# Moving the column maxima from TensorE to VectorE in a transformer block, and bunching the first MLP product

## The chip, the cores and the metric

The kernel runs on one core of a Trainium2 chip. The time is the device time of one execution in microseconds (us); lower is better. Several runs are taken and their median is used. One more execution is recorded by the hardware profiler; all spans, waits and durations below are from it. The engines are called by their names in the profile: PE (TensorE matmul), PEld (its weight loads), DVE (VectorE), ACT (ScalarE), POOL (GpSimd) and SP (SyncE, which here only issues DMAs).

## What is computed

A transformer block with conditioning, for 2 sequences of 2048 tokens, 576 channels, 16 heads of 36, all in fp32:

```python
ada = silu(c) @ W_ada + b_ada
shift_msa, scale_msa, gate_msa, shift_mlp, scale_mlp, gate_mlp = split(ada, 6)
h = layernorm(x) * (1 + scale_msa) + shift_msa
q, k, v = heads(h @ W_qkv + b_qkv)
o = softmax(q * 36 ** -0.5 @ k.T) @ v
x = x + gate_msa * (o @ W_proj + b_proj)
h = layernorm(x) * (1 + scale_mlp) + shift_mlp
x = x + gate_mlp * (gelu(h @ W_fc1 + b_fc1) @ W_fc2 + b_fc2)
```

The softmax needs, for each query, the maximum over 2048 keys. The MLP is 2304 wide, 18 chunks of 128.

## The kernel before

**Front.** The first part computes the conditioning rows in six parts (`rows_of`, products `pa`), and queries, keys and values of the first sequence. The generator `later` holds the conditioning parts 2 to 5 and the scaling of the projection weights by the gates. It is advanced by one `yield` for each step of the other work. Its bare `yield`s are all that sets where on PE the third part (`gates(2, g1)`, L425 on PE) stands.

**Main loop.** The attention is cut into 128 units, one for each head and each block of 512 queries (8 blocks of 16 heads). A unit has NG = 4 groups of 512 keys, and one turn of the loop, a slot, is one group. So slot g of a unit is one of 0 to 3. In slot G the loop emits, in this order:

- scores of the group eight slots ahead (`scores`, L648, 64x64 tiles, keys on the partitions, queries along the row), into two PSUM buffers of two banks, `ps_s`
- their copies to SBUF on ACT (`keep`, L661)
- filler on PE, if the slot is to have some (`fill`)
- the exponentials of the next slot's group on ACT (`exps`, L707)
- the last, 64-row part of the filler (`last`, `quads`, L104)
- weighting of the values with this slot's exponentials (`weigh`, L719, 64x64 tiles)
- on DVE the subtraction of the maximum from the group two slots ahead (`less`, L703) and the running maximum over keys of the new scores (`maxima`, L666)
- `flush()`, what was put off by a slot, then the eviction of the filler, then at a unit's last slot `take` (L731, L732), which adds the two halves of the weighted sum.

Every engine works through its instructions in the order written (`seq`). PE thus waits in `scores` for `keep` of the slot before, and in `weigh` for an exponential, which waits for a subtraction.

**The maximum.** After the fourth group, `acc` holds for each partition a maximum of each query over a part of the keys (twice 512 queries, folded into 512). What is left is a maximum across the 128 partitions. It is made one slot later (`chain`): `turn` transposes four 128x128 pieces on PE into one of the `ps_s` buffers (L684), `across` reduces them on DVE (L694), writes the 512 maxima to memory and reads them back spread over all partitions as `m` (L695, L698, both on SP's queue). The subtraction wants `m` two slots after that. SP's queue also carries the keys and queries of the next unit but one (`load_keys`, issued when a unit starts) and half of the stores of a unit's output (`store`).

**Filler.** What is not attention is cut into steps with a cost on PE: queries, keys and values of the second sequence (`projections`), and for each finished block the projection, the second norm and the MLP (`block`). Each slot adds RATE = 2.51 to a credit, each step takes its cost from it. Before, a slot takes a step if g is even, or if the credit is over RATE; the credit starts at -32. In the MLP, `up_to(f)` makes two chunks of the first product: four 128-row products for chunk 0 (cost 4.29, with the 64-row rest of both chunks), and, as a step of its own, four for chunk 1 (3.43). Then come the biases (L1183), a square (L1190), a DVE product (L1192), and one slot later tanh (L1198) and another product (L1200). `down` makes the second product (L1220, cost 5.94). These fillers use two PSUM banks, `ps_f`. The transposes of the normed tokens (`lights`) are put into slots that have no other filler.

**Closing loop.** When the last unit is done, the rest of the filler runs alone.

Of the kernel before, what the change touches and what calls it, by code (L numbers as in the profile page):

```python
# [10 lines left out]
F32 = mybir.dt.float32  # L11
AF = mybir.ActivationFunctionType
# [10 lines left out]
def dit_block_kernel(  # L23
# [150 lines left out]
    with ExitStack() as front:  # L174
# [342 lines left out]
        def later():  # L517

            was[2] = load_ada(2)
            was[5] = load_ada(5)  # L520
            lines = ap.tile([P, C], F32, name="lines")
            for b in range(B):
                for i, src in enumerate((b_fc2, b_proj)):
                    at = ds(64 * b + 32 * i, 1)
                    seq(nc.gpsimd.dma_start(out=lines[at, :], in_=src.unsqueeze(0)))
            yield
            yield
            yield
            pas[2] = cleared(2)
            yield  # L530
            g1 = []
            yield from gates(2, g1)
            was[3] = load_ada(3)
            pas[5] = cleared(5)
            yield
            g2 = []
            yield from gates(5, g2)
            was[4] = load_ada(4)
            half = [ap.tile([P, C], F32, name=f"half_{b}") for b in range(B)]
            for b in range(B):  # L540
                seq(nc.vector.tensor_scalar_mul(half[b], g2[b], 0.5))
                for i, (to, g) in enumerate(((gb_d, g2), (gp_d, g1))):
                    at = ds(64 * b + 32 * i, 1)
                    seq(nc.vector.tensor_mul(lines[at, :], lines[at, :], g[b][at, :]))
                    seq(nc.gpsimd.dma_start(out=to[b].unsqueeze(0), in_=lines[at, :]))
            yield
            split = lambda w: [
                (pieces(w)[0][:, kc : kc + 2, :], P, 2) for kc in range(0, KC - 1, 2)
            ] + [(w[(KC - 1) * P : C].unsqueeze(1), KL, 1)]
            to = [split(wpr_d[b]) for b in range(B)]  # L550
            jobs = [
                (*job, g1, [to[b][i][0] for b in range(B)])
                for i, job in enumerate(split(w_proj))
            ]
            src = w_fc2.rearrange("(f p) n -> p f n", p=P)
            dsts = [w2_d[b].rearrange("(f p) n -> p f n", p=P) for b in range(B)]
            for f in range(0, NF, 3):
                at = slice(f, f + 3)
                jobs.append((src[:, at, :], P, 3, half, [d[:, at, :] for d in dsts]))
            yield from gated(jobs)  # L560
            pas[3] = cleared(3)
            yield
            t = rows_of(3)
            pas[4] = cleared(4)
            yield
            modulation(3, t)()
            t = rows_of(4)
            yield
            modulation(4, t)()
# [29 lines left out]
    with ExitStack() as main_part:  # L599
# [12 lines left out]
        class Unit:  # L612
# [50 lines left out]
            def maxima(self, g):  # L663

                one, two = (self.es[g][:, j].rearrange("p i n -> p (i n)") for j in range(2))
                top = lambda out, x, y: seq(nc.vector.tensor_max(out, x, y))  # L666
                if g == 0:
                    self.acc = np_.tile([P, 2 * QB], F32, tag="acc", name=f"acc_{self.u}", bufs=1)
                    top(self.acc, one, two)
                    return  # L670
                a = self.acc
                top(a, a, one)
                top(a, a, two)
                if g == NG - 1:
                    self.am = a[:, :QB]
                    top(self.am, a[:, :QB], a[:, QB:])

            def turn(self):

                room = ps_s.tile([P, 2, 512], F32, tag="s", name=f"mt_{self.u}")  # L680
                self.pt = room[:, 0, :].rearrange("p (i n) -> p i n", i=TB)
                for i in range(TB):
                    seq(
                        nc.tensor.transpose(  # L684
                            self.pt[:, i, :],
                            self.am.rearrange("p (n i) -> p i n", i=TB)[:, i, :],
                            ident,
                        )
                    )

            def across(self):

                mx = np_.tile([P, TB], F32, tag="mx", name=f"mx_{self.u}")
                seq(nc.vector.tensor_reduce(out=mx, in_=self.pt, op=ALU.max, axis=AX.X))  # L694
                seq(nc.sync.dma_start(out=m_d[self.u], in_=mx))  # L695
                self.m = np_.tile([P, QB], F32, tag="m", name=f"m_{self.u}")
                flat = m_d[self.u].rearrange("p i -> (p i)")
                seq(nc.sync.dma_start(out=self.m, in_=flat.partition_broadcast(P)))  # L698

            def less(self, g):  # L700
# [417 lines left out]
        def block(k):  # L1118
# [36 lines left out]
            def up_to(f):  # L1155

                wc, wt = columns(w1s.pop(f))
                gT = mp.tile([P, 2, QB], F32, tag="gT", name=f"gT_{k}_{f}", bufs=5)
                gTs[f] = gT
                pfs = []  # L1160

                def last():

                    pfs.append(room(f"pf_{k}_{f}_1", 1)[0])
                    quads(pfs, wt, halves(h2, KC - 1), (False, True))

                for j in range(2):
                    if j == 0:
                        pfs.append(room(f"pf_{k}_{f}_0", 1)[0])
                    for kc in range(KC - 1):  # L1170
                        seq(
                            nc.tensor.matmul(  # L1172
                                pfs[j],
                                lhsT=wc[:, kc, ts(j, P)],
                                rhs=h2[:, kc, :],
                                start=(kc == 0 and j == 0),
                                stop=(kc == KC - 2 and j == 1),
                            )
                        )

                    def first(j=j):
                        seq(
                            nc.scalar.activation(  # L1183
                                gT[:, j, :], pfs[j], AF.Identity, bias=bias[:, ds(NQK + f + j, 1)]
                            )
                        )
                        if j == 0:
                            return
                        t = mp.tile([P, 2, QB], F32, tag="th", name=f"th_{k}_{f}", bufs=1)
                        seq(nc.scalar.activation(t, gT, AF.Square, scale=0.044715**0.5))  # L1190
                        seq(
                            nc.vector.scalar_tensor_tensor(  # L1192
                                t, t, 1.0, gT, op0=ALU.add, op1=ALU.mult
                            )
                        )

                        def second():
                            seq(nc.scalar.activation(t, t, AF.Tanh, scale=(2.0 / math.pi) ** 0.5))  # L1198
                            seq(
                                nc.vector.scalar_tensor_tensor(  # L1200
                                    gT, t, 1.0, gT, op0=ALU.add, op1=ALU.mult
                                )
                            )

                        later.append(second)

                    if j == 1 and f + 4 < NF:
                        w1s[f + 4] = load_w1(k, f + 4)
                    yield (4.29, first, last) if j == 0 else (3.43, first)

            def down(part):

# [80 lines left out]
        RATE = 2.51  # L1293
        lasts = []
        work = [[tokens(1, tb) if tb else None, projections(1, tb), None] for tb in range(NQB)]
        credit = -32.0
        state["busy"] = True
        units[0].kT, units[0].qT = first_keys

# [32 lines left out]
        for G in range(-AHEAD, NU * NG + 1):  # L1332
# [5 lines left out]
                units[su + 1].load_keys()  # L1338
            if g == 1 and -1 <= u and u + 1 < NU:
                units[u + 1].load_values()  # L1340
            cu, cg = divmod(G - 1 + AHEAD, NG)
            chain = cg == NG - 1 and 0 <= cu < NU
            count(RATE)
            forced = g % 2 == 0 or G < 0 or credit > RATE
            tiles = units[su].scores(sg) if su < NU else None
            if tiles:
                units[su].keep(sg, tiles)
# [6 lines left out]
            if 0 <= G + 1 < NU * NG:  # L1354
                lu, lg = divmod(G + 1, NG)
                units[lu].exps(lg)
            if chain:
                subtract(G + 2)
                units[cu].turn()
            for last in lasts:  # L1360
                last()
            lasts.clear()
            if 0 <= G < NU * NG:
                units[u].weigh(g)
            if chain:
                units[cu].across()
                if tiles:
                    units[su].maxima(sg)
            elif g == NG - 2:
                if tiles:  # L1370
                    units[su].maxima(sg)
                subtract(G + 2)
# [20 lines left out]
        while work:  # L1393
# [9 lines left out]
            for done in dones:  # L1403
                done()
            state["slot"] += 1
            for _ in range(1 + state["slot"] % 2):
                advance()


# [43 lines left out]
```

## Time and profile before

| | us |
|---|---|
| median of 3 runs (3703.10 to 3707.89) | 3703.63 |
| profiled execution | 3707.24 |
| its span, first to last instruction | 3705.5 |
| PE busy | 3682.3 |
| DVE busy | 2948.0 |
| ACT busy | 2327.3 |
| POOL busy | 706.2 |
| first scores of the main loop on PE | 269.65 |
| granted PE clock | 0.999 |

The span is what the shares refer to. A busy time is the time in which at least one instruction of that engine runs. A group of instructions is given as count, total busy time and mean duration of one; instructions of one engine overlap a little, so a duration is somewhat longer than the distance from one start to the next. "Idle before" is the time the engine stood still ahead of these instructions, with what ended it.

### The profile page before, as it was taken

How to read it: one execution, taken by the hardware profiler on the slowest of the kernel's cores; microseconds unless marked ns; L12 is line 12 of the kernel's file. 1: busy time of each engine (PE TensorE's matmuls, PEld its weight loads, DVE VectorE, ACT ScalarE, POOL GpSimd, SP SyncE). 2: the span in 40 equal slices, each digit the busy share in tenths (PEclk: the TensorE clock that was granted, in tenths of full speed). 3: DMA queues.
4: the chain of work that ended last, by engine and by line, in shares of the span. 5: the costliest groups of instructions: out<-in, count | busy, mean ns of one | idle time of the engine just before them, and what ended most of it. 6: DMA issues, size and time to landing. Idle time of an engine off the chain costs nothing.

```text
span 3705.5 us, 59239 instructions
## 1 busy us (share of the span) xinstructions
PE 3682.3 (99%) x23926; PEld 1722.0 (46%) x23926; DVE 2948.0 (80%) x3000; ACT 2327.3 (63%) x2166; POOL 706.2 (19%) x1044
## 2 busy tenths in 40 slices
PE   8999999999999999999999999999999999999999
PEld 4554344444444534454444444453444444444565
DVE  4627889889888888888889888988889888988422
ACT  0006767668776677667667777767667767676321
POOL 0101121222122111311131212211130213111411
PEclk9999999999999999999999999999999999999999
DMA  7733333544244343524353424424352435342522
GB/s 245 267 110 105 100 99 96 119 116 111 67 109 112 76 90 80 126 66 99 79 133 70 113 65 114 108 60 105 76 126 67 99 82 120 80 97 61 136 71 70
DMA packets 426946, 382.13 MB, mean 103 GB/s; under 512 B 315591, under 2 KB 316633, under 8 KB 426673
## 3 DMA queue, kind: packets, MB, share of 16 engines
q0 software_dynamic: 77248, 205.28, 20.5%
q1 hardware_dynamic: 82928, 129.54, 12.5%
q10 hardware_dynamic: 266496, 43.53, 7.2%
q8 instruction: 189, 3.10, 0.4%
q14 instruction: 85, 0.69, 0.1%
HBM read 306.98 MB, written 71.21 MB: 102 GB/s over the span
## 4 chain that ended last, share of the span: by engine, by line
PE 94%; DMA 3%; DVE 1%; ACT 1%; issue 1%; POOL 0%; SPq 0%; DVEq 0%; ACTq 0%; POOLq 0%
PE av L719 23%; PE s L648 22%; PE py L1220 15%; PE pf L1172 14%; PE po L799 4%; PE pq_q L975 3%; PE pq L278 3%; PE pf L104 2%; PE pv L328 2%; PE pv_q L799 2%; PE mt L684 2%; DMA x_b<-gp_d 1%; PE po L104 1%; DMA wa<-in_L_cond_W_ada_dram 1%; DVE acc L666 0%
## 5 line engine op out<-in xcount | busy, mean ns | idle before, releaser
L661 ACT COPY e<-s 128x1024 f32<-128x1024 f32 x1024 | 990.2, 1025 | 813.3 <-PE s L648 802.7
L703 DVE TENSOR_TENSOR e<-e,m 128x2048 f32<-128x2048 f32 x512 | 1162.8, 2276 | 9.8 <-DMA m<-m_d 9.8
L666 DVE TENSOR_TENSOR acc<-acc,e 128x1024 f32<-128x1024 f32 x768 | 939.5, 1223 | 171.9 <-ACT e L661 127.7
L707 ACT ACTIVATE e<-e 128x2048 f32<-128x2048 f32 x512 | 991.2, 1936 | 0.9 <-DVE e L703 0.8
L719 PE MATMUL av<-e,v 64*64 64x512 f32 x8192 | 981.3, 594 | 0.1
L648 PE MATMUL s<-qT,kT 36*64 36x512 f32 x8192 | 973.4, 589 | 2.1 <-DVE mx L694 1.1
L1220 PE MATMUL py<-w,gT 128*128 128x288 f32 x2304 | 580.2, 410 | 0.0
L648 PEld LDWEIGHTS s<-qT,kT 36*64 36x64 f32 x8192 | 313.1, 133 | 571.3 <-issue 522.8
L719 PEld LDWEIGHTS av<-e,v 64*64 64x64 f32 x8192 | 296.0, 133 | 510.0 <-issue 460.3
L1172 PE MATMUL pf<-h_b,w_b 128*128 128x512 f32 x1152 | 530.7, 605 | 0.0
L1220 PEld LDWEIGHTS py<-w,gT 128*128 128x128 f32 x2304 | 432.4, 190 | 175.4 <-issue 37.2
L740 POOL DMA_DIRECT2D o_d<-up x128 | 109.3, 854 | 1969.8 <-DMA o_d<-up 1439.2
L1172 PEld LDWEIGHTS pf<-h_b,w_b 128*128 128x128 f32 x1152 | 208.2, 190 | 318.0 <-issue 303.7
L694 DVE TENSOR_REDUCE mx<-mt 128x4 f32<-128x512 f32 x128 | 88.2, 689 | 169.9 <-PE mt L684 169.9
L1183 ACT ACTIVATE gT<-pf,bias 128x512 f32<-128x512 f32 x144 | 99.1, 688 | 193.0 <-PE pf L104 132.7
L1192 DVE SCALAR_TENSOR_TENSOR th<-th,gT 128x1024 f32<-128x1024 f32 x72 | 88.1, 1223 | 90.0 <-ACT th L1190 89.8
L666 DVE TENSOR_TENSOR acc<-e 128x1024 f32<-128x1024 f32 x128 | 155.6, 1216 | 4.4 <-ACT e L661 4.4
L1232 DVE TENSOR_TENSOR x_b<-py,x_b 128x288 f32<-128x288 f32 x192 | 81.5, 452 | 84.2 <-PE py L1220 84.2
L741 POOL DMA_DIRECT2D sum_d<-up x128 | 144.0, 1125 | 1.0 <-issue 1.0
L799 PE MATMUL po<-wpr_p,oT 128*128 128x288 f32 x512 | 132.6, 413 | 0.0
L278 PE MATMUL pq<-hT,w_in 128*128 128x512 f32 (+1 forms) x320 | 129.2, 555 | 0.0
L766 POOL DMA_DIRECT2D w_b<-in_L_cond_W_fc_dram x72 | 73.8, 1025 | 266.9 <-PE pf L1172 242.9
(156 smaller groups left out, 2453.2 us busy)
## 6 DMA issues: line engine op xcount, KB each, us to landing
w<-w_d POOLq DMA_DIRECT2D x72, 576.0 KB, 6.1
v<-v_d ACTq DMA_DIRECT2D x128, 296.0 KB
kT<-qk_d SPq DMA_DIRECT2D x256, 144.0 KB
w_b<-in_L_cond_W_fc_dram POOLq DMA_DIRECT2D x72, 512.0 KB, 4.6
m<-m_d SPq DMA_DIRECT2D x128, 256.0 KB
qT<-qk_d SPq DMA_DIRECT2D x256, 72.0 KB
w_d<-wg POOLq DMA_DIRECT2D x12, 864.0 KB, 8.4
qk_d<-ev SPq DMA_DIRECT2D x36, 256.0 KB
```

The costliest lines, as they stand in the source:

```text
L104: nc.tensor.matmul(outs[r][ts(c, 64), :], lhsT=lefts[r][:, ts(c, 64)], rhs=rights[r], start=starts[r], stop=not starts[r],)
L278: nc.tensor.matmul(pq[:, r, :n], lhsT=w_in[:, kc, cols], rhs=hT[:, kc, at], start=(kc == 0 and not (two and r)), stop=(kc == KC - 2 and tw ...
L648: nc.tensor.matmul(s[ts(c, 64), i, :], lhsT=self.kT[at, ds((2 * g + j) * P + 64 * c, 64)], rhs=self.qT[at, :], start=True, stop=True,)
L661: seq(nc.scalar.copy(self.es[g][:, j], s))
L666: top = lambda out, x, y: seq(nc.vector.tensor_max(out, x, y))
L703: seq(nc.vector.tensor_sub(e, e, m))
L707: seq(nc.scalar.activation(e, e, AF.Exp))
L719: nc.tensor.matmul(self.av[ts(i, 64), r, :], lhsT=self.v[ts(r, 64), ds((c + i * (HALF // P)) * HA, 64)], rhs=e[ts(r, 64), j, i, :], start= ...
L741: seq(nc.gpsimd.dma_start(out=sums, in_=hi[0:1, :], accum_op=ALU.add))
L799: nc.tensor.matmul(outs[n][:, :C2], lhsT=src[:, kc, ts(i, P)], rhs=w_[:, kc, ts(n, C2)], start=(kc == 0), stop=False,)
L1172: nc.tensor.matmul(pfs[j], lhsT=wc[:, kc, ts(j, P)], rhs=h2[:, kc, :], start=(kc == 0 and j == 0), stop=(kc == KC - 2 and j == 1),)
L1220: nc.tensor.matmul(py[n][:, :C2], lhsT=gTs[f - f % 2][:, f % 2, ts(i, P)], rhs=w2s[f - f % 2][:, f % 2, ts(n, C2)], start=(j == 0), stop=( ...
```

## The change

1. `turn` and `chain` go. The maximum across partitions is made on DVE alone, at once after the fourth group (in slot 3 instead of the next slot 0). DVE transposes 128x512 in squares of 32x32, reading with a step of 16 elements, reduces 128x(16x32) to 128x16, copies the four groups of 32 partitions side by side, and reduces over the four. The two DMAs follow as before, the first with 32 rows of 16 values instead of 128 of 4. On SP's queue they now stand ahead of the next `load_keys`.
2. `up_to` makes both chunks in one step of cost 7.72, each with its own bank from the start, and the rest of both after them.
3. A slot takes filler if g is 0, or in g = 2 if the credit is positive, or in g = 1 and 3 if it is over twice RATE. The credit starts at -34.
4. The third conditioning part comes two steps later (and with it what follows in `later`).
5. The closing loop advances the gathering of a block's outputs twice in each turn, instead of once and twice in turn.

```diff
             yield
+            yield
+            yield
             pas[2] = cleared(2)
...
                 if g == NG - 1:
-                    self.am = a[:, :QB]
-                    top(self.am, a[:, :QB], a[:, QB:])
-
-            def turn(self):
-                room = ps_s.tile([P, 2, 512], F32, tag="s", name=f"mt_{self.u}")
...
-            def across(self):
-                mx = np_.tile([P, TB], F32, tag="mx", name=f"mx_{self.u}")
-                seq(nc.vector.tensor_reduce(out=mx, in_=self.pt, op=ALU.max, axis=AX.X))
-                seq(nc.sync.dma_start(out=m_d[self.u], in_=mx))
+                    top(a[:, :QB], a[:, :QB], a[:, QB:])
+                    self.across(a)
+
+            def across(self, a):
+                v = a[:, QB:].rearrange("p (i n) -> p i n", n=32)
+                seq(nc.vector.transpose(v, a[:, :QB].rearrange("p (n i) -> p i n", n=32)))
+                n16 = QB // 32
+                mq = a[:, :n16]
+                seq(nc.vector.tensor_reduce(out=mq, in_=v, op=ALU.max, axis=AX.X))
+                m4 = a[:32, n16 : 5 * n16].rearrange("p (r i) -> p r i", r=4)
+                for r in range(4):
+                    seq(nc.vector.tensor_copy(m4[:, r], mq[ts(r, 32), :]))
+                mx = np_.tile([32, n16], F32, tag="mx", name=f"mx_{self.u}")
+                by_query = m4.rearrange("p r i -> p i r")
+                seq(nc.vector.tensor_reduce(out=mx, in_=by_query, op=ALU.max, axis=AX.X))
+                flat = m_d[self.u].rearrange("p i -> (p i)")
+                seq(nc.sync.dma_start(out=flat.rearrange("(n i) -> n i", n=32), in_=mx))
...
-                    if j == 1 and f + 4 < NF:
-                        w1s[f + 4] = load_w1(k, f + 4)
-                    yield (4.29, first, last) if j == 0 else (3.43, first)
+                if f + 4 < NF:
+                    w1s[f + 4] = load_w1(k, f + 4)
+                yield 7.72, first, last
...
-        credit = -32.0
+        credit = -34.0
...
-            forced = g % 2 == 0 or G < 0 or credit > RATE
+            forced = g == 0 or G < 0 or credit > (0.0 if g == 2 else 2 * RATE)
...
-            if chain:
-                subtract(G + 2)
-                units[cu].turn()
...
-            for _ in range(1 + state["slot"] % 2):
+            for _ in range(2):
```

## The prediction

> **What bounds the kernel now.** I read the busy times first, then the chain of waits, then the groups by line and shape, and then PE, ACT and DVE in order of time.
>
> ```profile
> PE 3682.3 (99%) x23926; PEld 1722.0 (46%) x23926; DVE 2948.0 (80%) x3000; ACT 2327.3 (63%) x2166; POOL 706.2 (19%) x1044
> PE 94%; DMA 3%; DVE 1%; ACT 1%; issue 1%; POOL 0%; SPq 0%; DVEq 0%; ACTq 0%; POOLq 0%
> ```
>
> PE is the bound, with 23 us of 3705.5 idle. So work taken off PE counts in full, until DVE at 80% or ACT at 63% makes PE wait.
>
> ```profile
> L703 DVE TENSOR_TENSOR e<-e,m 128x2048 f32<-128x2048 f32 x512 | 1162.8, 2276 | 9.8 <-DMA m<-m_d 9.8
> L666 DVE TENSOR_TENSOR acc<-acc,e 128x1024 f32<-128x1024 f32 x768 | 939.5, 1223 | 171.9 <-ACT e L661 127.7 <-DVE acc L666 0.9 <-ACT e L707 0.9
> L694 DVE TENSOR_REDUCE mx<-mt 128x4 f32<-128x512 f32 x128 | 88.2, 689 | 169.9 <-PE mt L684 169.9
> ```
>
> DVE's largest idle groups are the maxima waiting for the copies out of PSUM (127.7) and the reduction waiting for PE's transposes (169.9). The second disappears with the transposes. The chain in order of time prices PE (start, us, what):
>
> ```profile
> 211.80 3.43 PE pq L278 x8
> ...
> 365.30 1.88 PE av L719 x16
> ...
> 372.98 0.47 PE mt L684 x4
> ...
> 381.71 3.63 PE pq_q L975 x8
> 385.34 1.02 PE pq_q L104 x8
> 386.36 1.72 PE av L719 x16
> ```
>
> One group of scores or of weighting is 1.72 us. Four 128-row products are 3.43 among their own kind (first row) and 3.63 after 64x64 ones. Weighting is 1.88 where it follows 128-row work. So going from 64x64 tiles to the full array costs 0.18 to 0.20 us and coming back 0.16, 0.34 for the round trip. Summing both orders of instructions with these prices gives 3431 us from the first scores (269.65) to the end of the kernel before. The profile leaves 3436 there, so in the main loop PE hardly ever waits. The last prices are those of ACT around a finished pair of the MLP's first product, and of DVE:
>
> ```profile
> 2250.38 0.69 ACT L1183 ACTIVATE gT<-pf,bias 128x512 f32<-128x512 f32 x1 [0.48 <-PE pf L1172]
> 2251.11 1.06 ACT L1190 ACTIVATE th<-gT 128x1024 f32<-128x1024 f32 x1
> 2253.15 1.93 ACT L661 COPY e<-s 128x1024 f32<-128x1024 f32 x2 [0.98 <-PE s L648]
> 2254.96 1.92 ACT L707 ACTIVATE e<-e 128x2048 f32<-128x2048 f32 x1
> 2256.77 1.06 ACT L1198 ACTIVATE th<-th 128x1024 f32<-128x1024 f32 x1
> ```
>
> From start to start two copies take 1.81 and an exponential 1.81. One group without filler costs PE 3.44 but ACT 3.62.
>
> The front has one wait of PE, in PE's rows in order of time:
>
> ```profile
> 40.81 3.66 PE L425 MATMUL pa<-wa,cT 128*2 128x288 f32 x20 [3.11 <-DMA wa<-in_L_cond_W_ada_dram]
> ```
>
> And DVE by windows (length, busy): a plain unit of the start, here DVE alone, and 400 us of the blocks, with PE, weight loads, DVE, ACT and POOL in turn:
>
> ```profile
> 467.30:490.60 23.30, 19.80 (x16) 1.00 0.43 97
> 1900.00:2300.00 400.00, 400.00 (x2735) 182.94 (x2734) 347.27 (x321) 282.52 (x258) 78.91 (x117) 1.00 0.40 96
> ```
>
> **Taken off PE.** (1) Four transposes per unit, 128 units: 128 x 0.47 = 60 us. They stood beside 128-row filler or added switches counted next. (2) The order of the changed kernel has 521 changes of tile shape from the first scores on, against 641: 60 round trips x 0.34 = 20 us. The pairs whose second chunk now follows the first directly account for them. (3) The third conditioning part: PE waits 3.11 us at 37.7 for its weights. Moved two steps on, it stands behind some 8 us of products whose operands are there (the weights land at 40.7). That gives 3 us, 0 if something in the front takes its place. Its DMAs are issued where they were; the later parts' loads and the weight scaling on POOL's queue move two steps, about 8 us, and are wanted after hundreds. Together -83.
>
> **Added to DVE.** The old reduction (0.69) goes. A transpose 128x512, a reduction of the same size, four copies 32x16 and a reduction to 32x16 come; I call their sum X. The trace has no DVE transpose. Its nearest rows are 128x512 instructions at 0.69. The lower bound is that less some overlap (0.6), the upper one the row of twice the elements (1.22), since it reads with a step of 16 elements, which no row here does. I take 0.7. The second reduction is the old row, 0.69. Dependent small instructions of the row statistics start every 0.20 us, a memset of 128x27 takes 0.08. So the copies cost 0.3 to 0.8; I take 0.8, as they depend on one another's quadrants like the statistics on their values. The last reduction is 0.2. X = 2.4, bounds 1.8 to 3.0.
>
> The Trainium skill, "SBUF — State Buffer", section "Door 1: The DMA port swizzle" (its note on cachelines), speaks against this transpose: a pattern that moves to a new 16-byte line with each fp32 element pays a penalty. No row here shows it. "VectorE: DVE Perf Modes", section "The three transpose paths", has a 128x128 bf16 block transpose at 311 ns; an estimate from it at one element a cycle would be 0.7 us again, so X would stay, while the cacheline rule, read as half the rate, would put X at 2.9.
>
> Nothing on PE waits for X itself: the maximum of a unit is wanted by the subtraction three slots later, behind 11.2 us of DVE's own queue (sum of up 0.6, two subtractions 4.4, five maxima 6.2). The way through memory took some 9 before, and DVE waited for m 9.8 us in all; were that cover gone, such waits would come to DVE, not to PE. In the timeline the store of the maxima is followed by the load of m after 1.4 to 5.9 us. But on SP the keys of the next unit but one, and then the stores of the last unit, now queue behind that load. The keys have some 3 us left; 0 to 8 us over the run, I take 0.
>
> **Added by the bunching.** Filler now comes in slot 0 of a unit always, in slot 2 only with credit, and a pair is 7.7 us. The order shows 44 places where a slot with filler is followed by three without. Before, there was never more than one in a row.
>
> (a) 28 follow a pair. Count from the filler's end. ACT: two biases (0.11, 0.67), square at 1.40 (DVE's product from 2.5), copies 2.88, exponential 4.69, tanh 6.50, copies 7.45, exponential 9.26, done 11.2. PE, with weighting and scores of 1.72 in turn, wants that exponential for the third weighting at 10.4. It waits 0.9 with the signal: 28 x 0.9 = 25 us. Bounds: 0 if ACT's earlier pieces have slid forward, 1.5 if DVE is late with the subtraction too (that is due at 9.3 and done at 5.9). The nine after the second product lack bias, square and tanh: 10.3 against 10.4, nothing.
>
> (b) The other seven, with one place where transposes fill the short slots, are eight units in a row, right after the start, for the credit starts lower and only slot 0 is served. PE needs 150 us for them. DVE without X: 19.8 - 0.69 = 19.1 per unit as in the row above (467.30), 153; four evictions of values 3.6 (eight sums at 0.45), statistics of one token block 6.4 (8 x 0.37, 4 x 0.21, 13 small ones at 0.2), X 8 x 2.4 = 19: 182. DVE may fall about 5 us behind before a subtraction is late for its exponential. PE waits 27 to 28 us. With X 1.8 and 10 us of slack it is 17, with 3.0 and 2 us 35.
>
> In the blocks the window from 1900 to 2300 is nearly 16 units: DVE 347 - 11 + 16 x 2.4 = 375 of PE's new 392, and a unit with three empty slots puts it back by about 1 us, which the next unit gives back. Nothing there.
>
> **Costed at nothing.** A pair takes both filler banks at once; the next filler starts at least 3.4 us after it, the biases have emptied them by 1.4. The loads of the first product's weights still leave after a pair's last product; the pair after next starts 15 us later, 7.8 in the closing loop, against 7.2 for three issues (1.03 and twice 0.76) and a landing of 4.6: 0.6 us to spare, as before. The closing loop advances the gathering twice per step, but a step that was two is one; the lower credit leaves it 6 us more filler, which PE only does later, as PE is busy there too (252 of the last 255 us).
>
> **Sum.** -83 + 25 + 28 = -30 us. The profiled execution took 3707.24 (span 3705.5), 3.6 above the median; from it the sum is 3677, from the median 3703.63 it is **3674**, which I predict. Its own range, from the bounds of (a) and (b): -83 + 0 + 17 to -83 + 42 + 35, so 3638 to 3698.
>
> **Rivals.** *The waits don't come*: PE has queues full of work and DVE loses 170 us of waiting on the transposes, so ACT and DVE run further ahead than I grant, and only PE's saving shows. 3620. Against it: exponentials follow copies on ACT in order, and PE's two score buffers keep ACT from running ahead. Chance 0.19. *DVE becomes the bound*: the transposition with its step, or the small copies, cost more than my bounds, X = 3.3. Then a block has 336 + 53 = 389 us of DVE work; half of the waits that remain (products for squares 89.8 and second-product sums 84.2 over 7.5 blocks) add 12, 401 against 392, 9 x 6.5 = 59; (b) is 35, (a) 25: -83 + 119 = +36, 3740. It decides from X = 2.9 on. For it: DVE is at 87% in the blocks. Against: no 128x512 row is over 0.81. Chance 0.17. *The gain is just eaten*: X near 2.9, within 0.2% (7.4 us, about what a measurement here can tell from no change), 0.08. The forecast keeps 0.56.
>
> **Numbers.** Faster by over 0.2%: 0.56 + 0.19 = 0.75; within: 0.08; slower: 0.17. The range goes from 3630 (half of the first rival, which spreads around 3620 to 3640) to 3712 (between no change and the second rival).
>
> **What would show it.** The transposes' group is gone, PE's busy time without waits near 3600, DVE's idle time on mt gone. The transpose row at 0.7, its copies at 0.2 from start to start. PE's weight loads of av wait for exponentials some 50 us, where 30.3 stood, half of it between 310 and 480 us, with DVE there over 95% busy. The wait at 40.8 us gone. I am wrong if DVE shows 95% over the blocks, if scores wait for kT, or if the eight early units take 19 us each.

## The result, and the profile after

| | before | after |
|---|---|---|
| median of 5 runs, us | 3705.88 | 3812.61 |
| lowest to highest | 3703.1 to 3711.14 | 3810.22 to 3828.98 |
| span of the profiled execution | 3705.5 | 3809.9 |
| granted PE clock | 0.999 | 0.988 |
| one block of 16 units (below) | 400.7 | 411.3 |

The changed kernel is slower: ratio 1.03, 95% interval 1.0275 to 1.0325. The time of a block is taken from the sums that end a unit (`up`): from that of the 32nd unit to that of the 112th there are five blocks, 1082.3 to 3085.8 us before and 1117.4 to 3173.8 after.

The page after, busy times and the group of weightings (count, busy, mean ns of one, idle before and what ended it):

```profile
PE 3654.1 (96%) x23414; PEld 1646.6 (43%) x23414; DVE 3202.8 (84%) x3768; ACT 2318.7 (61%) x2166; POOL 705.5 (19%) x1044
L719 PE MATMUL av<-e,v 64*64 64x512 f32 x8192 | 1007.4, 608 | 136.0 <-DVE up L732 113.1
```

PE is 28.2 us less busy than before, but idle for 155.8 us where 23.2 stood: 132.6 - 28.2 = 104.4, the whole difference of the spans. Most of the new idle time has one name, the sum `up` on DVE; the kernel before has no such wait. PE's longest waits after (who waits, line, what it waits for, then total us, times, longest):

```profile
PE av L719 <- DVE up L732: 113.1, 66, 5.9
PE av L719 <- ACT e L707: 22.7, 31, 1.7
PE pa L425 <- DMA wa<-in_L_cond_W_ada_dram: 4.6, 2, 4.4
```

A unit's weighting goes into one PSUM accumulator, `av`, whose pool holds one. `take` empties it: ACT copies the one half, DVE adds the other (`up`, L732). The next unit's first weighting writes there again, so it waits for that addition. This is DVE in order of time around such a place (start, us, what), and then PE:

```profile
2365.56 2.23 DVE L703 TENSOR_TENSOR e<-e,m 128x2048 f32<-128x2048 f32 x1
2367.70 2.54 DVE L668 TENSOR_TENSOR acc<-acc,e 128x1024 f32<-128x1024 f32 x2
2370.28 0.69 DVE L668 TENSOR_TENSOR acc<-acc 128x512 f32<-128x512 f32 x1
2371.00 1.03 DVE L685 STREAM_TRANSPOSE acc<-acc 128x512 f32<-128x512 f32 x1
2372.07 0.69 DVE L688 TENSOR_REDUCE acc<-acc 128x16 f32<-128x512 f32 x1
2372.79 0.69 DVE L691 COPY acc<-acc 32x16 f32<-32x16 f32 x4
2373.52 0.25 DVE L694 TENSOR_REDUCE mx<-acc 32x16 f32<-32x64 f32 x1
2373.72 0.69 DVE L732 TENSOR_TENSOR up<-up,av 128x512 f32<-128x512 f32 x1
2374.33 2.29 DVE L703 TENSOR_TENSOR e<-e,m 128x2048 f32<-128x2048 f32 x1
```

```profile
2360.36 1.95 PE L719 MATMUL av<-e,v 64*64 64x512 f32 x16 [0.70 <-ACT e L707]
2362.13 1.90 PE L650 MATMUL s<-qT,kT 36*64 36x512 f32 x16
2363.95 6.09 PE L1212 MATMUL py<-w,gT 128*128 128x288 f32 x24
2374.47 3.69 PE L719 MATMUL av<-e,v 64*64 64x512 f32 x16 [4.42 <-DVE up L732]
```

Two things are to be seen. DVE never stands still here, and from 2371.00 to 2373.72 everything it does is new: 2.72 us that the addition stands behind. Without them it could have started at 2371.00, and PE's wait, by an estimate from these rows, would have been 1.7 us. PE had finished the unit's last weighting at 2362.3, scores and filler at 2370.0, and waits 4.42 us. And after the wait the same 16 matmuls take 3.69 us in place of 1.95.

The new DVE work by groups:

```profile
L685 DVE STREAM_TRANSPOSE acc<-acc 128x512 f32<-128x512 f32 x128 | 135.6, 1059 | 4.4
L688 DVE TENSOR_REDUCE acc<-acc 128x16 f32<-128x512 f32 x128 | 87.8, 686 | 4.4
L691 DVE COPY acc<-acc 32x16 f32<-32x16 f32 x512 | 85.4, 167 | 9.6
L694 DVE TENSOR_REDUCE mx<-acc 32x16 f32<-32x64 f32 x128 | 31.7, 248 | 4.4
```

The windows (length, then busy times of PE, weight loads, DVE, ACT and POOL, granted clock), after, in the blocks and in the early units; then the early window of before:

```profile
1900.00:2300.00 400.00, 385.39 (x2628) 169.24 (x2621) 370.57 (x412) 274.95 (x253) 76.60 (x112) 0.99 0.38 94
400.00:500.00 100.00, 83.76 (x584) 29.03 (x582) 95.77 (x117) 72.17 (x68) 12.57 (x18) 0.93 0.28 73
```

```profile
400.00:500.00 100.00, 99.23 (x706) 41.31 (x699) 89.65 (x93) 77.33 (x74) 18.09 (x26) 1.00 0.36 92
```

In the blocks DVE is at 93%, not full, and PE stands still 14.6 us of 400. Of the 113.1 us of waits on the sum, 63.3 lie in the five blocks and 23.5 between 300 and 600 us.

### The profile page after: what moved, and what is told of

Same layout as the page of the kernel before. It is cut to its first block, busy times and chain, and to the rows that moved or that the text cites. A ratio compares the mean times of both kernels' runs of the same rounds, so it can differ in the third digit from the quotient of the medians.

```text
span 3809.9 us, 58893 instructions
## 1 busy us (share of the span) xinstructions
PE 3654.1 (96%) x23414; PEld 1646.6 (43%) x23414; DVE 3202.8 (84%) x3768; ACT 2318.7 (61%) x2166; POOL 705.5 (19%) x1044
## 5 line engine op out<-in xcount | busy, mean ns | idle before, releaser
L719 PE MATMUL av<-e,v 64*64 64x512 f32 x8192 | 1007.4, 608 | 136.0 <-DVE up L732 113.1
L650 PE MATMUL s<-qT,kT 36*64 36x512 f32 x8192 | 986.2, 596 | 2.1 <-ACT e L663 1.1
L1165 PE MATMUL pf<-h_b,w_b 128*128 128x512 f32 x1152 | 513.3, 598 | 1.6 <-DVE x_b L1224 1.6
L1181 ACT ACTIVATE gT<-pf,bias 128x512 f32<-128x512 f32 x144 | 91.2, 684 | 335.3 <-PE pf L104 335.3
L766 POOL DMA_DIRECT2D w_b<-in_L_cond_W_fc_dram x72 | 64.7, 899 | 554.8 <-PE pf L104 450.6
L668 DVE TENSOR_TENSOR acc<-e 128x1024 f32<-128x1024 f32 x128 | 155.8, 1217 | 4.4 <-ACT e L663 4.4
L685 DVE STREAM_TRANSPOSE acc<-acc 128x512 f32<-128x512 f32 x128 | 135.6, 1059 | 4.4
```

The source lines that it names most:

```text
L650: nc.tensor.matmul(s[ts(c, 64), i, :], lhsT=self.kT[at, ds((2 * g + j) * P + 64 * c, 64)], rhs=self.qT[at, :], start=True, stop=True,)
L685: seq(nc.vector.transpose(v, a[:, :QB].rearrange("p (n i) -> p i n", n=32)))
L719: nc.tensor.matmul(self.av[ts(i, 64), r, :], lhsT=self.v[ts(r, 64), ds((c + i * (HALF // P)) * HA, 64)], rhs=e[ts(r, 64), j, i, :], start= ...
L1165: nc.tensor.matmul(pfs[j], lhsT=wc[:, kc, ts(j, P)], rhs=h2[:, kc, :], start=(kc == 0), stop=False,)
```

## The experiments

Three theories. **A**: the accumulator is held, because the sum that empties it stands behind the new work in DVE's queue. **B**: DVE has too much work in all, wherever it stands. **C**: the three empty slots in a row, which the bunching makes, are the cause. Ratios are to the kernel before on the same chip, with 95% intervals. The runs were on several chips, on which the kernel before took 3705.85 to 3709.85 us, so a difference between two times in us can be off by some 4. A wait "on the sum" is one of PE's on `up`.

**e1, the work behind the sum.** The changed kernel, with `across` called after `take`:

```diff
-                    self.across(a)
...
                 units[u].take()
+            if tiles and sg == NG - 1:
+                units[su].across(units[su].acc)
             advance()
```

> The changed kernel with one thing moved: the steps across the partitions stand behind the sum `up` in DVE's queue instead of ahead of it. Theory A (the one PSUM accumulator of the weighting is held, because `up`, which empties it, queues behind 2.8 us of new DVE work): PE's 113 us of waits for up go, and with them most of the slow clock, so 3640 to 3690. Theory B (DVE simply has too much work): the waits move to the exponentials and the time stays over 3780. Theory C (three slots without filler in a row let DVE fall behind, and the accumulator is only where it shows): half of it at most comes back, 3740 to 3790.

3714.75 us, 1.0014 [1.0005, 1.0023]. PE's waits:

```profile
PE av L718 <- DVE up L731: 38.7, 20, 5.7
PE av L718 <- ACT e L706: 23.9, 33, 1.7
```

DVE does the same work (3181.2 us busy against 3202.8), only the sum now stands ahead of it in the queue, and 98 us come back. In the five blocks the waits on the sum fall from 63.3 us to 16.0, and a block from 411.3 us to 397.9. Of the 38.7 that remain, 17.2 lie between 300 and 600 us.

**e2, ACT empties both halves.** The changed kernel, with `across` in its place:

```diff
-                seq(nc.vector.tensor_add(self.up, self.up, self.av[:, 1, :]))
+                second = self.v[:, :QB]
+                seq(nc.scalar.copy(second, self.av[:, 1, :]))
+                seq(nc.vector.tensor_add(self.up, self.up, second))
```

> The changed kernel, but ACT copies both halves of the accumulator out of PSUM (0.6 us more of ACT per unit) and DVE adds them from SBUF. DVE's queue is as in the changed kernel. Theory A: PE no longer waits for up, 3640 to 3700. Theories B and C: DVE is as late as before and the subtractions with it, over 3780.

3722.84 us, 1.004 [1.0026, 1.0054].

```profile
PE av L719 <- ACT e L707: 26.8, 36, 2.0
PE s L650 <- ACT e L663: 20.6, 20, 2.3
```

No wait on the sum is left, and 90 us come back though DVE's work stays where it was. The price is the second line: ACT, with one more copy per unit, is late with the copies of scores. Two different edits that free the accumulator thus recover nearly the same.

**e3, no bunching.** The kernel before, with the maxima made on DVE ahead of the sum, but single chunks, the old rule for filler and the old credit.

```diff
-                    self.am = a[:, :QB]
-                    top(self.am, a[:, :QB], a[:, QB:])
...
+                    top(a[:, :QB], a[:, :QB], a[:, QB:])
+                    self.across(a)
...
```

> The kernel before with only the maxima turned on DVE, in the changed kernel's place ahead of up; filler rule, pairs, credit and front as before. Theory A: PE saves 60 us of transposes and still waits for up where DVE is behind, 3660 to 3750, with a PE wait for up in the trace. Theory C: no row of empty slots, so no waits, 3640 to 3650. Theory B: 3780 or more.

3762.52 us, 1.0143 [1.0128, 1.0159].

```profile
PE av L717 <- DVE up L730: 90.7, 61, 5.5
```

So the waits on the sum need no run of empty slots, which rules out C as their cause.

**e4, the bunching alone.** The kernel before with parts 2 and 3 of the change, the transposes still on PE.

```diff
...
-        credit = -32.0
+        credit = -34.0
...
-            forced = g % 2 == 0 or G < 0 or credit > RATE
+            forced = g == 0 or G < 0 or credit > (0.0 if g == 2 else 2 * RATE)
```

> The kernel before with only the bunching (both chunks in one step, the new rule, credit -34); maxima as before on PE. Theory A: no wait for up, 22 us of waits for exponentials against 20 us of saved changes of tile shape, so 3695 to 3725. Theory C: 3750 or more. Theory B: 3680 to 3700.

3745.86 us, 1.0098 [1.0083, 1.0113].

```profile
PE av L719 <- ACT e L707: 22.7, 31, 1.7
PE mt L684 <- DVE acc L666: 12.7, 8, 6.5
PE pt_b L863 <- ACT xn_b L838: 7.2, 4, 5.4
```

There is no wait on the sum. The waits on exponentials, 22.7 us, stand for the 25 that the prediction had for three empty slots; the changed kernel has the same row. The other two lines are not in the changed kernel: `mt` is the old transposes, and `pt_b`, transposes of normed tokens in the filler, shows again in e15 (7.2 us in 4 places), where the transposes are off PE. I read that line as one of when filler falls due. A block takes 401.8 us, and the time lies above A's figure (3695 to 3725).

**e5, the maxima behind the sum, no bunching.** As e3, with `across` after `take` as in e1.

> The kernel before with only the maxima turned on DVE, standing behind up (filler rule, pairs, credit, front as before). Theory A (the accumulator is held by work that stands ahead of up): against the same with the work ahead of up (3762) the 91 us of waits and most of the slow clock go, 3645 to 3670, and faster than before by the 60 us of transposes less small change. Theory B (DVE has too much work): not under 3700.

3689.69 us, 0.9957 [0.9943, 0.9972]: faster than both kernels.

```profile
PE av L716 <- DVE up L729: 30.0, 31, 2.6
```

Two things follow. In all three pairs the bunching costs time: 36 us with the transposes on PE (e4), 25 behind the sum (e1 against e5), 50 ahead of it (the changed kernel against e3; in the last two pairs it comes with parts 4 and 5). And A's figures were missed in e1, e2, e3 and e5, by 12 to 25 us each: less came back than A said, so it is not the whole loss. e9 comes back to this.

**e6, pairs under the old rule.** As e5, with both chunks in one step.

> As the run before with both chunks of the first product in one step, under the old rule and credit. Pairs as such harmless: another 10 to 20 us less from the fewer changes of tile shape, 3630 to 3660. If the pair itself brings waits (three empty slots, exponentials late): 3660 to 3700.

3874.47 us, 1.0455 [1.0438, 1.0473], far above both figures expected.

```profile
PE av L716 <- DVE up L729: 77.3, 23, 6.8
PE pt_b L860 <- ACT xn_b L835: 68.9, 28, 9.0
PE po L796 <- DVE oT L1081: 29.5, 4, 26.6
```

PE takes transposes and the projection before their inputs are there (68.9 and 29.5 us). That the old rule, which gives two steps to a unit whatever they cost, runs ahead of the blocks' results is my reading; the waits are what the trace shows. The new rule and the pairs belong together.

**e7 and e8, a measured load.** The kernel before, transposes on PE, with four idle 128x512 maxima per unit (2.79 us) ahead of the sum (e7) or behind it (e8):

```diff
+                    for _ in range(4):
+                        top(a[:, QB:], a[:, QB:], a[:, QB:])
```

> The kernel before, nothing moved, but at the end of a unit's maxima DVE repeats a 128x512 maximum four times on a half of acc that nobody reads (2.6 to 2.9 us per unit), ahead of up. Theory A: PE waits for up, 60 to 110 us more, 3770 to 3815. Theory B: the same whether ahead or behind.

> The same four repeats, behind up in DVE's queue. Theory A: little, 3705 to 3730. Theory B: as much as ahead.

3826.28 us, 1.0322 [1.0306, 1.0337], and 3832.1, 1.0338 [1.0323, 1.0354]. The place made next to no difference here, as B had it. Ahead, PE waits on the sum for 72.6 us. Behind, it waits for something else:

```profile
PE s L648 <- DVE mx L694: 72.7, 48, 3.0
...
PE av L719 <- DVE up L732: 1.5, 2, 0.8
```

While the transposes are on PE, the old reduction `mx` empties a buffer that scores need. The load behind the sum stands ahead of that reduction. So "behind the sum" is no safe place as such; safe is a place with no release of a PSUM buffer soon after it.

**e9, the new work left out.** The changed kernel without transposition, first reduction and copies: what is left out is the maximum across partitions.

```diff
-                seq(nc.vector.transpose(v, a[:, :QB].rearrange("p (n i) -> p i n", n=32)))
-                seq(nc.vector.tensor_reduce(out=mq, in_=v, op=ALU.max, axis=AX.X))
-                for r in range(4):
-                    seq(nc.vector.tensor_copy(m4[:, r], mq[ts(r, 32), :]))
```

> The changed kernel without transposition, reduction and the four copies (left out: the maximum across the partitions; the last reduction takes 32 rows of the running maxima as they are, and the values that are subtracted are these). DVE has 2.44 us a unit less ahead of the sum that empties the accumulator, 312 us in all. Theory A (accumulator held): PE's waits on that sum fall from 113 us to under 25. What remains against the kernel before is then the bunching without DVE's new work: by the prediction's own terms -83 + 25 + about 10 = -48, 3657 us; by the bunching as it was measured alone (+36, with the transposes still on PE) less the transposes' 60 and the front's 3, 3678 us. The difference to the run with DVE's work behind the sum (3714.75) is what this work costs even there: over 30 us if the load of DVE as such counts (B), under 10 if only the place does.

3663.53 us, 0.9878 [0.9862, 0.9894]. The page, and PE's waits:

```profile
PE 3606.8 (99%) x23414; PEld 1641.3 (45%) x23414; DVE 2899.5 (79%) x3000; ACT 2317.4 (63%) x2166; POOL 706.8 (19%) x1044
```

```profile
PE av L713 <- ACT e L701: 22.7, 31, 1.7
PE av L713 <- DVE up L726: 11.0, 8, 5.5
```

The prediction's terms without the new DVE work give 3657; a block takes 393.2 us, for which the prediction had 392. So PE's saving and the bunching were priced well. All the rest of the changed kernel, 3812.6 - 3663.5 = 149 us, is the price of some 2.4 us of DVE work per unit. e1 splits it: 98 for the place, 51 that stay behind the sum. A and B thus both hold, A for about two thirds. The two are not strictly apart: of the 51, 28 are still waits on the sum (38.7 in e1, 11.0 here), which DVE reaches late, and 17 are longer busy time of PE (3624.3 against 3606.8).

**e10, e11, e12, places and helpers**, all on e5. e10 puts the work behind the first subtraction of the next slot. e11 adds part 4 of the change, the later third conditioning part; e12 adds that and e2's emptying by ACT.

> The kernel before with the maxima on DVE in the place where the old reduction stood: after the first subtraction of the next unit's first slot, 2 us behind the sum that empties the accumulator and ahead of that slot's maxima. Old filler rule, no pairs. Theory A: PE's waits on the sum are as few as where the work stood right behind the sum (30.0 us) or fewer, and the time is 3690 us or a few us less, since the subtraction no longer waits for the maxima. Rival (late maximum): the way through memory starts 2 us later, and DVE waits for m; then DVE's idle time on m is over 100 us and the time 3700 to 3720.

> The kernel before with the maxima on DVE behind the sum, as in the run that took 3689.69, and the third conditioning part two steps later. By the prediction PE's wait of 3.1 us at 40.8 goes and nothing takes its place: 3686.6 us. Rival: the wait moves to the next instruction that wants memory, 3689 to 3691.

> As the run with the later third part, and ACT copies both halves of the accumulator, so that DVE adds from SBUF and PE waits for ACT alone. Theory A: the 30 us of PE's waits on the sum fall to under 5, and DVE has 0.24 us a unit less; in their place ACT has 0.7 us a unit more, in the changed kernel 21 us of waits of the scores on ACT's copies. So 3670 to 3682 if the waits on the sum were real cost, 3690 to 3705 if ACT, which has more ahead of the copies of scores, holds PE instead.

e10: 3715.63 us, 1.0022 [1.0011, 1.0033], waits on the sum 41.2 us, longest 4.3; DVE waits 3.6 us for m, so neither theory has its figure right. These waits explain 11 of the 18 us by which its profiled execution is longer than that of e5; the rest I have not settled. e11: 3691.74, 0.9947 [0.9933, 0.9961]; e12: 3692.63, 0.9953 [0.994, 0.9966]. These two and e5 can't be told apart. In e12 no wait on the sum is left, where e11 has 26.5 us, but others have taken their place:

```profile
PE po L800 <- DVE x_b L1110: 12.1, 8, 3.0
PE py L1221 <- DVE x_b L1110: 8.4, 3, 5.1
```

So these waits were no reserve: PE then waits for DVE in the filler. That is B, at DVE's 86%.

**e13, only the copies left out.** The changed kernel without the maximum over the four groups of partitions.

> The changed kernel without the four copies (left out: the maximum over the four groups of partitions; the last reduction takes 32 rows of running maxima). DVE has 2.07 us a unit of new work ahead of the sum in place of 2.76. If the price goes by the length of what stands ahead of the sum, evenly, the two runs known (0.32 us: 3663.5; 2.76 us: 3812.6) give 61 us of time for each us, so 3770. If there is a slack that is free and the price steep behind it, it is 3710 to 3740. If it is the copies between groups of partitions that are dear by themselves, 3680 or less.

3743.53 us, 1.0093 [1.0077, 1.0108]; the waits on the sum are 65.6 us in 41 places. The trace has the new work, from its first start to that of the sum, at 1.87 us (median of the units where the sum follows directly), not the 2.07 of the expectation; in e9 it is 0.21, in the changed kernel 2.75. From 0.21 to 1.87 it is 80 us of time, 48 for each us; the last 0.88 cost 69, 78 for each us. Neither end of the expectation is right: there is no free slack, and the price climbs.

**e14, a read in order.** As e5, the transposition without its step of 16, and so 4-byte pieces in memory:

```diff
-                seq(nc.vector.transpose(v, a[:, :QB].rearrange("p (n i) -> p i n", n=32)))
+                seq(nc.vector.transpose(v, a[:, :QB].rearrange("p (i n) -> p i n", n=32)))
...
-                seq(nc.sync.dma_start(out=flat.rearrange("(n i) -> n i", n=32), in_=mx))
+                seq(nc.sync.dma_start(out=flat.rearrange("(i n) -> n i", n=32), in_=mx))
```

> As the run that took 3689.69 (old filler rule, maxima on DVE behind the sum), and the transposition reads its 128x512 in order, not with a step of 16; the 512 maxima then go to memory in pieces of 4 bytes in place of 64. The transposition takes 0.69 us in place of 1.06: 0.37 x 128 = 47 us less DVE work; behind the sum the new work cost 51 us for 312, so 8 us of time: 3682. Rivals: the step costs nothing and the transposition stays at 1.06, 3690; the store in small pieces is slow and m late, DVE waits on m for over 50 us, 3700 or more.

3819.72 us, 1.0302 [1.0282, 1.0322]: the third rival.

```profile
L700 DVE TENSOR_TENSOR e<-e,m 128x2048 f32<-128x2048 f32 x512 | 1160.2, 2272 | 120.2 <-DMA m<-m_d 119.7
L682 DVE STREAM_TRANSPOSE acc<-acc 128x512 f32<-128x512 f32 x128 | 90.2, 704 | 0.1
```

The transposition is 0.70 us as predicted, so the step made it 1.06. But the subtractions now wait 119.7 us for m, and so DVE is late for PE, which waits 69.1 us on the sum where e5 has 30.0. The step, with the 64-byte pieces that it allows, buys a maximum that is there in time.

**e15, a higher start credit.** As e1, with the credit at -18.

> As the run of the changed kernel with the work behind the sum (3714.75), and the credit starts at -18 in place of -34, so that six more slots of the early units have filler and PE has work while DVE catches up. That run lost 19 us by its sixteenth unit against the one without the work (694 us after the start against 674). If the empty slots there are the cause, 3700 to 3705. Rival: the filler is missing later and the loss moves to the end, 3710 to 3720.

3748.54 us, 1.0109 [1.0092, 1.0126], above both ranges expected. The sixteenth unit's sum is at 702 us (e1: 693), so the early units gained nothing, and a block takes 403.3 us, waits on the sum 54.4. The credit also sets which steps fall beside which unit in the blocks; why this order is so much worse I have not settled.

A second accumulator in PSUM was not tried.

## Why the prediction was wrong

**The step that failed** is the sentence "Nothing on PE waits for X itself". It asked who wants the maximum, and found slack of 11.2 us. That part is true: m made DVE wait 1.7 us in the changed kernel. It did not ask who wants the instructions that stand behind the maximum's. The addition of `take` does, and it releases PE's only accumulator. e1 and e2 show it: one moves that release ahead, the other to another engine, and 98 and 90 of the 107 us come back. e9 shows the whole price: without the work 149 us are gone.

**Blocks, "Nothing there".** The load was priced well: 375 us of DVE for PE's 392, and with X as measured 347 - 11 + 16 x 2.76 = 380; the window shows 370.57 of 400, 381 for a block of 411.3. The conclusion was wrong: 63.3 us of waits on the sum stand there. A mean of 95 to 97% left no slack at a release that comes each unit. In e1, with that release ahead of the new work, DVE still costs 397.9 - 393.2 = 4.7 us per block.

**X.** Predicted 2.4, measured 2.76 (2.72 at the place shown): the transposition 1.06, not 0.7. The upper bound, 1.22, held it. The Trainium skill's "SBUF — State Buffer", "Door 1: The DMA port swizzle", which warned of patterns that move to a new 16-byte line with each element, fits in that there is a price; e14 has it at 1.06 to 0.70, a factor of 1.5, not the half rate that I read into it. That the lines are its reason no run here shows.

**Off PE.** PE's busy time without waits was to be near 3600; e9, with the same matmuls, has 3606.8. So transposes and changes of shape together took off 75.5 us where the prediction had 80; no run parts the two.

**Front.** The wait of 3.1 us is gone, and the first scores come at 264.95, not 269.65. But e5, with the old front, has that wait at 0.47 and its first scores at 267.21, and e11, with the new one, at 266.93. In the traces of the nine kernels with the old front the first scores come at 266.2 to 271.1 (median 267.2), in the eight with the new one at 264.8 to 267.0 (median 265.5). So the edit is worth 1 or 2 us rather than 3, and the times (3689.69, 3691.74) show no gain.

**(a)** 25 us predicted, 28 places of 0.9; measured 22.7, 31 places of 0.73, and the same in e4 and e9, where e5, without the bunching, has 0.7. Right. The sign given for it was not: PE's weight loads of av wait 89.6 us for exponentials, not some 50.

**(b)** The early units were to cost 27 to 28 us. Between 300 and 600 us PE waits 23.5 us on the sum, and DVE is at 96% in the middle third of it. Place and size were near; what PE waited for was the sum, not the exponential. In e9, without the new work, 9.9 of these remain.

**The clock** was not in the sum. The changed kernel and e9 issue the same 23414 matmuls, but PE is busy 3654.1 us in one and 3606.8 in the other: the granted clock is 0.988 and 0.999, and 40 of these 47 us are in the weightings and the scores, the instructions behind the waits. From e9 to the changed kernel the waits on the sum grow by 113.1 - 11.0 = 102.1 us, and with the 47 this makes 149, all that parts them. Against the prediction's own 3674, the 47 and some 90 us of waits on the sum outside the early units give 3811; that this meets 3812.6 so closely is partly luck, for other terms were off as well (75.5 us for 80, 22.7 for 25).

**Rivals.** "DVE becomes the bound" was on the right side, with the wrong threshold: X at 2.76 lies below the 2.9 from which it was to decide, for it too looked at the mean. "The waits don't come" falls: they came. "The gain is just eaten" falls too, X being near its figure and the loss 3%. None of the three signs of being wrong came either (DVE is at 93% over the blocks, no scores wait for kT, the early units take 23.5 us each): all of them look at means or at other buffers.

## What to carry to other kernels

Before you add work to an engine's queue, list what stands behind the new instructions up to the next release of a buffer that exists once, and ask who waits for that; who wants the new result is only half of the question. DVE, at 93 to 96% in the stages here, had no slack for a release that comes in every turn: the first 1.7 us ahead of it cost 48 us of time for each us per unit, the next 0.9 cost 78. Where the work must go there, put it behind the release (3689.69 us here with the old filler, 0.43% faster than before), and check that no other release then stands behind it (e8). And price each part of a change by itself: the bunching, by the prediction's own terms 25 + 28 - 20 = 33 us dearer, cost time in every pair.

## What the runs showed of the hardware

- After a long wait PE runs slower. In the changed kernel 96 weightings of 16 matmuls follow a wait on the sum or an exponential. Up to 2.0 us of waiting, all 69 take 1.95 us. From 2.0 to 2.6, nine take 1.95 and six 2.63 to 3.64; the three from 2.6 to 3.0 take 2.68 to 3.31. Over 3 us, seven of nine take 3.69 and two about 2.7. These rows alone add up to 24 of the 47 us; in all the weightings are 26.5 us longer than in e9, the scores 13.7. The Trainium skill, "TensorE: Matmul & The Clock Gate", section "What's actually happening", has the clock halved after an idle window of about 3.4 us that runs freely. The longest times, 3.69 to 1.95, come near that; but waits from 2.04 us on already show slower matmuls, and not all of these do.
- A transposition in 32x32 squares of 128x512 fp32 takes 0.70 us read in order, 1.06 with a step of 16 elements (704 ns in e14, 1052 in e5).
- A copy of 32x16 from one group of 32 partitions to another takes 0.167 us, four of them 0.69 from the first start to the last end.
